# Edge softmax by products over edges, an attention table in two parts, and a new order of the last layers, in a four-layer graph network

## The chip, the cores and the metric

The kernel runs on one core of one Trainium2 chip. The core has five engines with instruction streams of their own, which wait for one another by semaphores: TensorE (PE in the profile; PEld are its weight loads), VectorE (DVE), ScalarE (ACT), GpSimd (POOL) and SyncE (SP). SP and POOL here mostly issue transfers between DRAM and on-chip memory (SBUF); a queue's transfers are issued in program order, so one that has to wait holds up those behind it. Products of TensorE land in PSUM. The metric is the device time of one execution in microseconds (us); less is better.

## The reference, cut to what matters

Input `x` is [128, 64, 256]: 128 samples of 64 nodes with 256 features. Four layers each compute `x = layernorm(x + layer(x))`: two graph convolutions with windows of LSTMs, a graph convolution with batch norm, attention over 512 random edges, and a convolution in the eigenvector basis of the graph. The change is in the last two and in the tables of the third:

```
def _L2_gnn_ref(H, W_lin, W_val, a, W_out, A0, src, dst):     # 4 heads of 64, E = 512 edges
    Xq, Xv = (H @ W_lin.T), (H @ W_val.T)                     # each as [bt, 64, 4, 64]
    e = einsum('behd,hd->beh', leaky_relu(Xq[:, src] + Xq[:, dst], 0.2), a)
    e = e + log(A0[src, dst] + EPS)
    m = segment_max(e_t, src, 64)                             # per source node
    ex = exp(e_t - m[src])
    denom = segment_sum(ex, src, 64)
    attn = ex / denom[src]
    Y = segment_sum(attn * Xv[:, dst], src, 64)
    return Y @ W_out.T

def _L3_gnn_ref(features, A, W1, b1, W2, b2):
    _, U = eigh(normalized Laplacian of A)
    h = relu(U.T @ features @ W1 + b1)
    return U @ (h @ W2 + b2)
```

## The kernel before, in words

**Where things are.** X, the activations, stays in SBUF as [128, 64 tiles, 256]: a tile holds two samples (b = 0, 1), each with its 64 nodes on 64 partitions. All layers update X in place. `Norm` (L1221) is the residual and layer norm: `add` adds a result to two tiles and takes their statistics on VectorE; when four tiles are gathered, `flush` works out the scale and shift in some ten small operations (a square root of them on ScalarE, L1214) and ScalarE applies them, one instruction a tile (L1253).

**Attention, scores.** `scores()` is a generator of 32 steps; step k covers two tiles. A step has two half-steps c = 0, 1 (two of the four heads each): TensorE gathers source plus target by a product with the 0/1 table GG (`l`, L1903), ScalarE copies it out (L1909), VectorE makes the leaky ReLU (L1910), TensorE multiplies by the attention vector into the score tile `sc` (L1857), maps the next tiles to queries and values (`m`, L1880), and transposes those after (L1869). Values are stored to DRAM by SP, one `xv` store a step (L1884). Sixteen steps are a half: 32 tiles give a score tile of 128 rows (16 units of two tiles, two parities, two heads) by 512 edges for each c.

**Softmax of a half.** Edges are sorted by source, so the reference's segments are runs of columns. `softmax(half, es)` runs on VectorE: add the edge logs `lg`; for each c two scans over the 512 columns (forward and backward, L1932 and L1933) spread each run's maximum, with `br` breaking them at the runs' ends; subtract; exponential on ScalarE; two more scans (L1937, L1938) with the 0/1 table `kp` (1 where a column goes on with the run) spread each run's sum; a reciprocal of 128x512 (L1940); a product (L1941). Each `yield` is a place where the hand-written order can put other work.

**Table.** `table` transposes the result into edges by rows on TensorE (L1951), copies it to `at` on ScalarE in an order that puts each parity's 128 values side by side (L1952), and scatters 4 x 128 edge rows of 1 KB with four indirect transfers from POOL (L1955) into `attn_d`, a DRAM table [64 x 64 pairs, 256] that was filled with zeros long before (L1740). Each scatter waits until the one before has landed. `fetch(half)` reads that table back into `M2` [128, 64, 128] with eight transfers from SP (L1964); each row that is read contiguously is one pair's 128 floats of one parity, 512 B.

**Values.** `values()` is a generator of 33 calls. Call k loads the next unit (`load`: ScalarE copies a slice of M2 to `mc`, L1971; POOL fetches the stored values `xr`, L1974), multiplies attention by values for two tiles (`mixed`, L1986), copies `yT` (L1989), and does the output product of the tiles before (`po`, L2007) with `ln.add`. So every second call closes four tiles of X with a flush. Calls that load units 0 to 15 read the first half's M2, the others the second's.

**The last layer.** `blocks()` is a generator of 19 calls; call q does basis(q) (L2074: four tiles times U, ScalarE copies `ag`, POOL adds the constant `cb` to X at L2078), first_map(q − 1) (L2084), back(q − 2) (L2092) and second_map(q − 3) (L2101, then `ln3.add` and the store of four finished tiles by SP, L2103). basis(q) needs tiles 4q to 4q + 3 of X after attention's norm. `constants()` prepares `cb` and `nb` from four small loads (L2046 to L2052), once (L2057).

**The order** is written out by hand in `run(...)`, which takes one step of each generator named; the streams of the engines follow it, with the scheduling tools of the language free to move little. In before, the softmax of half 0 is laid beside five steps of scoring, `table` follows, and `fetch(0)` one step later; four steps of scoring on come seven pairs of a scoring step and a value call. After scoring: the loads of the last layer's weights, `constants()`, value calls mixed with the softmax of half 1 and blocks, and the table of half 1; then

```
fetch(1)
run(*[val, val, l3] * 10)
run(*[val] * 2, *[l3] * (NT // 4))
```

The source's own line numbers are those of the profile.

Of the kernel before, what the change touches and what calls it, by code (L numbers as in the profile page):

```python
# [1259 lines left out]
def tile_adj_resnorm(ctx: ExitStack, tc: tile.TileContext, I: dict, out: bass.AP, layers: int = 4):  # L1260
# [45 lines left out]
    EDGE = (("GG", E), ("lg", E), ("kp", E + 1), ("br", E + 1), ("ix", 4))  # L1306
# [4 lines left out]
    attn_d = dram.tile([N * N + E, 2 * P], F32, tag="attn_d", name="attn_d")  # L1311

    def edge_tables(t):
        at, o = 0, {}
        for name, w in EDGE:
            o[name] = t[:, at : at + w]
            at += w
        return [o[k] for k in ("GG", "lg", "kp", "br")] + [o["ix"].bitcast(I32)]
# [73 lines left out]
    def sort_edges(gk, gp):  # L1392

        def gt_(tag, shape, dtype=F32, bufs=None):
            return gk.tile(shape, dtype, tag=tag, name=tag, bufs=bufs)

        edge_s = gt_("edge_s", [P, WE])
        GG, lg, kp, br, ix = edge_tables(edge_s)
# [54 lines left out]
        v.memset(kp, 0.0)  # L1453
        v.tensor_tensor(kp[:, 1:E], row[0][:, 1:], row[0][:, : E - 1], ALU.is_equal)
        v.tensor_scalar(br, kp, 1.0, 1e30, ALU.subtract, ALU.mult)
        OS, OD = gt_("kr", [P, E]), gt_("ef", [P, E])
        v.tensor_scalar(OS, row[0], pmod, None, ALU.is_equal)
        v.tensor_scalar(OD, row[1], pmod, None, ALU.is_equal)
        v.tensor_tensor(GG, OS, OD, ALU.add)
        ps = gp.tile([P, 512], F32, tag="ps", name="ps")  # L1460
# [278 lines left out]
    for z in attn_d[: N * N, :].rearrange("(k p a) q -> k p (a q)", p=P, a=4):  # L1739
        nc.sync.dma_start(z, zero)  # L1740
# [65 lines left out]
    with ExitStack() as l2:  # L1806
# [9 lines left out]
        GG, lg, kp, br, ix = edge_tables(edge_s)  # L1816
# [16 lines left out]
        kf, kb, bf, bb = kp[:, :E], kp[:, 1:], br[:, :E], br[:, 1:]  # L1833
# [6 lines left out]
        es, soft = [[], []], []  # L1840
# [83 lines left out]
        def softmax(half, es):  # L1924

            for c in range(2):
                es.append(sm.tile([P, E], F32, tag="se", name="se"))
                v.tensor_tensor(es[c], sc[half][c], lg, ALU.add)
            yield
            for c, e in enumerate(es):  # L1930
                f = sm.tile([P, 2, E], F32, tag="sf", name="sf", bufs=1)[:, 0, :]
# [5 lines left out]
                v.tensor_tensor_scan(f, kf, e, 0.0, ALU.mult, ALU.add)  # L1937
                v.tensor_tensor_scan(f[:, ::-1], kb[:, ::-1], f[:, ::-1], 0.0, ALU.mult, ALU.max)  # L1938
                yield
                v.reciprocal(f, f)  # L1940
                v.tensor_tensor(e, e, f, ALU.mult)  # L1941
                yield

        def table(es):

            at = sm.tile([P, 2, E], F32, tag="sf", name="at", bufs=1).rearrange(
                "p a b -> p (a b)").rearrange("p (k b u c i) -> p k b u c i", k=4, b=2, u=HU, c=2)
            for c, e in enumerate(es):
                ps = pp.tile([P, 512], F32, tag="m", name="m")
                for k in range(4):  # L1950
                    te.transpose(ps[:, k * P : (k + 1) * P], e[:, k * P : (k + 1) * P], ident)  # L1951
                s.copy(at[:, :, :, :, c, :].rearrange("p k b u i -> p (k b) i u"),  # L1952
                       ps.rearrange("p (k i u) -> p k i u", i=4, u=HU))
            for k in range(4):
                nc.gpsimd.indirect_dma_start(  # L1955
                    out=attn_d[:, :], out_offset=bass.IndirectOffsetOnAxis(ap=ix[:, k : k + 1], axis=0),
                    in_=at[:, k].rearrange("p b u c i -> p (b u c i)"), in_offset=None)

        def fetch(half):

            M2[half] = lw.tile([P, N, P], F32, tag="M2", name="M2", bufs=2)
            for n0 in range(0, N, 16):
                for b in range(2):
                    nc.sync.dma_start(  # L1964
                        M2[half][b * N : (b + 1) * N, n0 : n0 + 16, :],
                        attn_d[: N * N, b * P : (b + 1) * P].rearrange("(d n) q -> d n q", n=N)[:, n0 : n0 + 16, :])
# [44 lines left out]
        def run(*steps):  # L2011
            for x in steps:
                next(x, None)
# [7 lines left out]
        lw, sm = own1(valuing, name="l2w", bufs=1), own1(valuing, name="l2s", bufs=2)  # L2021
        ln = Norm(nc, sm, X, 4, act=True)
        val = values()
        soft += [softmax(h, es[h]) for h in range(2)]
# [14 lines left out]
        with tc.tile_pool(name="l3w", bufs=1) as l3w, tc.tile_pool(name="l3s", bufs=2) as s3, tc.tile_pool(  # L2039
            name="l3p", bufs=6, space=PSUM  # L2040
        ) as p3:
            bank = lambda: p3.tile([P, 512], F32, tag="ps", name="ps")
            w1 = l3w.tile([P, 2, P], F32, tag="w31", name="w31")
            nc.sync.dma_start(w1, kio(I["W31"]))
            w2 = l3w.tile([P, D], F32, tag="w32", name="w32")
            nc.sync.dma_start(w2, I["W32"])  # L2046
            b1 = l3w.tile([P, 1], F32, tag="b31", name="b31")
            nc.sync.dma_start(b1, I["b31"])
            nb1 = l3w.tile([P, P], F32, tag="nb1", name="nb1")
            nc.sync.dma_start(nb1, I["b31"].rearrange("p o -> (p o)").partition_broadcast(P))  # L2050
            cb = l3w.tile([P, D], F32, tag="cb", name="cb")
            nc.sync.dma_start(cb, I["b32"].partition_broadcast(P).rearrange("p o d -> p (o d)"))  # L2052

            def constants():
                v.tensor_scalar(nb1, nb1, -1.0, None, ALU.mult)
                ps = bank()
                te.matmul(ps[:, :D], b1.to_broadcast([P, P]), w2, start=True, stop=True)  # L2057
                te.matmul(ps[:, D : D + 1], bdut, ones[:, 0:1], start=True, stop=True)
                ru = l3w.tile([P, 1], F32, tag="ru", name="ru")
                v.tensor_copy(ru, ps[:, D : D + 1])  # L2060
                v.tensor_tensor(cb, cb, ps[:, :D], ALU.add)
                v.tensor_scalar(cb, cb, ru, None, ALU.mult)

# [121 lines left out]
```

## Time and profile before

| what | value |
|---|---|
| median of 3 runs | 2470.07 us (2470.02 to 2470.59) |
| the profiled execution | 2471.62 us, of which the span of the trace 2469.8 |
| granted TensorE clock, mean | .977 |
| ScalarE busy | 964.4 us (39%) |
| GpSimd busy | 75.1 us (3%) |
| DMA | 101.25 MB, mean 41 GB/s |
| softmax of half 0, first to last VectorE operation | about 2050 to 2090 us |
| scores end | about 2256 us |
| softmax of half 1 | 2252.8 to 2290.3 us |
| eight indirect scatters, issue each | .96 to 1.02 us; landing 2.4 to 3.6 us |
| sixteen reads of the table, landing each | 5.5 to 14.6 us |

Times in the timeline are from the start of the span. A timeline row has a start, a duration, engine, line, operation, destination and sources, a count where several of a kind follow one another, and in brackets how long the engine had been idle and what released it. A windows row has a length, and then, in the order PE, PEld, DVE, ACT, POOL, the busy us in it with the number of instructions; after these the granted clock of TensorE (1.00 is full), the mean busy share of the 16 DMA engines and the GB/s moved. A tile row has the shortest, median and longest duration in ns, and the first and last start.

### The profile page before, as it was taken

How to read it: one execution, taken by the hardware profiler on the slowest of the kernel's cores; microseconds unless marked ns; L12 is line 12 of the kernel's file. 1: busy time of each engine (PE TensorE's matmuls, PEld its weight loads, DVE VectorE, ACT ScalarE, POOL GpSimd, SP SyncE). 2: the span in 40 equal slices, each digit the busy share in tenths (PEclk: the TensorE clock that was granted, in tenths of full speed). 3: DMA queues.
4: the chain of work that ended last, by engine and by line, in shares of the span. 5: the costliest groups of instructions: out<-in, count | busy, mean ns of one | idle time of the engine just before them, and what ended most of it. 6: DMA issues, size and time to landing. Idle time of an engine off the chain costs nothing. (4 is left out here: it accounts for less than half of the span.)

```text
span 2469.8 us, 29195 instructions
## 1 busy us (share of the span) xinstructions
PE 2300.6 (93%) x9016; PEld 1232.0 (50%) x9016; DVE 1794.5 (73%) x8172; ACT 964.4 (39%) x1678; POOL 75.1 (3%) x115
## 2 busy tenths in 40 slices
PE   7999999999999999999999988998978888899797
PEld 5544654444664444655445634554433333246786
DVE  3667766677977798877889877777846768456577
ACT  1322222242332343322333322334447665456575
POOL 0000000000000000000000000000000000002331
PEclk9999999999999999999999999999989999999899
DMA  6000000000100001000001001002210000511622
GB/s 213 18 18 35 1 34 1 34 26 9 52 35 1 35 35 51 1 35 1 35 34 52 1 29 36 35 1 111 75 37 22 22 22 22 98 35 47 133 87 74
DMA packets 59861, 101.25 MB, mean 41 GB/s; under 512 B 5137, under 2 KB 40081, under 8 KB 59441
## 3 DMA queue, kind: packets, MB, share of 16 engines
q1 hardware_dynamic: 54624, 88.83, 11.3%
q0 software_dynamic: 3216, 10.21, 1.5%
q8 instruction: 72, 1.18, 0.2%
q14 instruction: 93, 0.75, 0.1%
q10 hardware_dynamic: 1856, 0.28, 0.1%
HBM read 67.84 MB, written 31.46 MB: 40 GB/s over the span
## 5 line engine op out<-in xcount | busy, mean ns | idle before, releaser
L1587 PE MATMUL pq<-H,wi 128*128 128x512 f32 (+1 forms) x2016 | 826.8, 546 | 5.1 <-DVE H L1612 5.1
L1593 ACT ACTIVATE gate<-pq,bl 128x512 f32<-128x512 f32 (+1 forms) x504 | 317.7, 635 | 845.9 <-PE pq L1591 663.1
L1587 PEld LDWEIGHTS pq<-H,wi 128*128 128x128 f32 x2016 | 373.4, 190 | 333.2 <-issue 260.1
L1591 PE MATMUL pq<-lh,wh 128*128 128x512 f32 (+1 forms) x1152 | 474.8, 538 | 24.9 <-DVE lh L1608 24.6
L1591 PEld LDWEIGHTS pq<-lh,wh 128*128 128x128 f32 x1152 | 216.1, 192 | 223.2 <-issue 138.7
L1910 DVE SCALAR_TENSOR_TENSOR xs<-xs 128x512 f32<-128x512 f32 x256 | 166.2, 681 | 67.6 <-ACT xs L1909 66.9
L1909 ACT COPY xs<-l 128x512 f32<-128x512 f32 x256 | 137.2, 589 | 85.4 <-PE l L1903 45.4
L1903 PE MATMUL l<-edge_s,xq 64*128 64x512 f32 x512 | 140.3, 648 | 16.4 <-ACT xs L1909 11.6
L1733 PE MATMUL ps<-at,w 128*128 128x512 f32 x256 | 116.7, 607 | 9.2 <-ACT at L1729 7.7
L1880 PE MATMUL m<-wqv,xT 128*128 128x512 f32 x256 | 123.1, 618 | 1.7 <-ACT xs L1909 0.9
L1750 PE MATMUL ps<-h,w 128*128 128x512 f32 x256 | 114.6, 606 | 5.9 <-ACT h L1745 5.9
L1605 ACT ACTIVATE gate<-lc 128x1024 f32<-128x1024 f32 (+1 forms) x72 | 69.0, 958 | 119.6 <-DVE lc L1600 61.8
L1253 ACT ACTIVATE X<-X,ln_sh,ln_rs 128x256 f32<-128x256 f32 x192 | 99.1, 590 | 25.5 <-DVE ln_sh L1249 19.7
L142 DVE COPY AQR<-eps 64x192 f32<-64x192 f32 (+1 forms) x125 | 35.1, 281 | 101.9 <-PE eps L148 101.7
L1237 DVE BATCH_NORM_STATS2 ln_st<-X 128x6 f32<-128x256 f32 x256 | 98.9, 415 | 2.2
L1880 PEld LDWEIGHTS m<-wqv,xT 128*128 128x128 f32 x256 | 46.0, 192 | 78.1 <-issue 58.6
L1903 PEld LDWEIGHTS l<-edge_s,xq 64*128 64x128 f32 x512 | 47.9, 196 | 69.9 <-issue 35.6
L1750 PEld LDWEIGHTS ps<-h,w 128*128 128x128 f32 x256 | 48.9, 194 | 66.2 <-issue 57.5
L1733 PEld LDWEIGHTS ps<-at,w 128*128 128x128 f32 x256 | 47.6, 192 | 65.7 <-issue 48.6
L1974 POOL DMA_DIRECT2D xr<-xv x32 | 17.6, 550 | 2053.7 <-DVE xs L1910 1836.4
L1857 PE MATMUL sc<-xs,az 128*32 128x512 f32 x512 | 68.2, 605 | 3.0 <-DVE xs L1910 3.0
L1602 DVE TENSOR_TENSOR gate<-gate 128x1024 f32<-128x1024 f32 (+1 forms) x36 | 38.0, 1055 | 42.7 <-ACT gate L1593 42.7
(557 smaller groups left out, 3222.2 us busy)
## 6 DMA issues: line engine op xcount, KB each, us to landing
wi<-in_WihT_dram SPq DMA_DIRECT2D x16, 1024.0 KB, 4.8
wh<-in_WhhT_dram SPq DMA_DIRECT2D x12, 1024.0 KB, 6.5
X<-in_x_dram SPq DMA_DIRECT2D x16, 512.0 KB, 9.2
xd<-X SPq DMA_DIRECT2D x16, 512.0 KB, 2.6
X<-xd SPq DMA_DIRECT2D x16, 512.0 KB, 3.2
xv<-xv SPq DMA_DIRECT2D x32, 256.0 KB, 2.0
xr<-xv POOLq DMA_DIRECT2D x32, 256.0 KB, 2.9
M<-attn_d SPq DMA_DIRECT2D x16, 512.0 KB, 11.2
```

The source lines that it names most:

```text
L1237: nc.vector.bn_stats(st, self.X[:, k, :])
L1253: nc.scalar.activation(x, x, AF.Identity, bias=sh[:, k : k + 1], scale=rs[:, k : k + 1])
L1587: te.matmul(ps, wi[:, kk, o * P : (o + 1) * P], at(kk, k), start=(kk == 0), stop=(k == 0 and kk == 1))
L1591: te.matmul(ps, wh[:, kk, o * P : (o + 1) * P], hst[:, kk, :M], start=False, stop=(kk == 1))
L1593: s.activation(gates[gt][:, c, :M], ps, AF.Tanh if gt == 2 else AF.Sigmoid, bias=bl[:, p - 1, o : o + 1])
L1605: s.activation(gg, cs2, AF.Tanh)
L1733: te.matmul(ps, w1[:, k, c * P : (c + 1) * P], at[:, k, :], start=(k == 0), stop=(k == 1))
L1750: te.matmul(ps, w2[:, k, c * P : (c + 1) * P], h[:, k, :], start=(k == 0), stop=(k == 3))
L1880: te.matmul(ps, xT[:, i, c, :], wqv[:, c, :], start=(c == 0), stop=(c == 1))
L1903: mms.append(te.matmul(pl[i][:, b, :], xq[i][r, c * P : (c + 1) * P], GG[r, :], start=True, stop=True))
L1909: taken.append(s.copy(x, pl[i][:, b, :]))
L1910: ready.append(v.scalar_tensor_tensor(x, x, 0.2, x, ALU.mult, ALU.max))
```

## The change

*Tables of the edges* (set up early, in layer 0): `kp` goes; `OS` comes, 0/1 of source node (128 rows, the 64 nodes twice) by 512 edges, which GG was already made from, and `OE`, its transpose in four pieces of 128 edges by 64 nodes, made by four transposes and a copy.

*Softmax*: the maxima stay as scans. The sums and their inverses are made after the transposition: the exponentials are transposed as before and copied to `eT` unpermuted; four products over edges with OE give the sums per node [64, 128]; VectorE bounds them from below by .5 and takes their reciprocal; four products with OS spread these back over the edges; VectorE multiplies `eT` by that, writing `at` in the permuted order. `table` is now the end of the same generator, which has eight steps in all.

*Table*: one DRAM table for each parity, each [pairs, 128]. There are eight scatters with rows of 512 B, in two chains. `fetch` reads, for a target node, 16 pairs x 128 floats that lie together: 8 KB.

*Order*: softmax 0 is laid beside six steps of scoring with `fetch(0)` after the sixth; three steps of scoring and `constants()` (its loads now go out before the steps around the middle of scoring, and its weights have a pool of their own), then the seven pairs as before. After scoring, seven blocks instead of six come before the first value call that reads the second table, and the repeated period starts with the block.

```diff
-    EDGE = (("GG", E), ("lg", E), ("kp", E + 1), ("br", E + 1), ("ix", 4))
+    EDGE = (("GG", E), ("OS", E), ("lg", E), ("br", E + 1), ("OE", 4 * N), ("ix", 4))
-    attn_d = dram.tile([N * N + E, 2 * P], F32, tag="attn_d", name="attn_d")
+    attn_d = [dram.tile([N * N + E, P], F32, tag=f"attn_d{b}", name="attn_d") for b in range(2)]
...
+        for k in range(4):
+            te.transpose(ps[:, k * N : (k + 1) * N], OS[:N, k * P : (k + 1) * P], ident[:N, :N])
+        v.tensor_copy(OE, ps[:, : 4 * N])
...
-    for z in attn_d[: N * N, :].rearrange("(k p a) q -> k p (a q)", p=P, a=4):
-        nc.sync.dma_start(z, zero)
+    for b in range(2):
+        for z in attn_d[b][: N * N, :].rearrange("(k p a) q -> k p (a q)", p=P, a=8):
+            nc.sync.dma_start(z, zero)
...
                 s.activation(e, e, AF.Exp)
                 yield
-                v.tensor_tensor_scan(f, kf, e, 0.0, ALU.mult, ALU.add)
-                v.tensor_tensor_scan(f[:, ::-1], kb[:, ::-1], f[:, ::-1], 0.0, ALU.mult, ALU.max)
-                yield
-                v.reciprocal(f, f)
-                v.tensor_tensor(e, e, f, ALU.mult)
-                yield
...
+            byedge = []
+            for e in es:
                 ps = pp.tile([P, 512], F32, tag="m", name="m")
                 for k in range(4):
                     te.transpose(ps[:, k * P : (k + 1) * P], e[:, k * P : (k + 1) * P], ident)
-                s.copy(at[:, :, :, :, c, :].rearrange("p k b u i -> p (k b) i u"),
-                       ps.rearrange("p (k i u) -> p k i u", i=4, u=HU))
+                eT = sm.tile([P, 4, P], F32, tag="sf", name="eT")
+                s.copy(eT.rearrange("p k r -> p (k r)"), ps)
+                ps = pp.tile([P, 512], F32, tag="m", name="m")
+                for k in range(4):
+                    te.matmul(ps[:N, :P], OE[:, k * N : (k + 1) * N], eT[:, k, :], start=(k == 0), stop=(k == 3))
+                rc = sm.tile([N, P], F32, tag="rc", name="rc")
+                v.tensor_scalar(rc, ps[:N, :P], 0.5, None, ALU.max)
+                v.reciprocal(rc, rc)
+                byedge.append((eT, rc))
+                yield
...
+            for c, (eT, rc) in enumerate(byedge):
+                ps = pp.tile([P, 512], F32, tag="m", name="m")
+                for k in range(4):
+                    te.matmul(ps[:, k * P : (k + 1) * P], OS[:N, k * P : (k + 1) * P], rc, start=True, stop=True)
+                v.tensor_tensor(at[:, :, :, :, c, :].rearrange("p k b u i -> p (k b) i u"),
+                                eT.rearrange("p k (i u) -> p k i u", u=HU).rearrange("p k (b i) u -> p (k b) i u", b=2),
+                                ps.rearrange("p (k i u) -> p k i u", i=4, u=HU), ALU.mult)
+                yield
             for k in range(4):
-                nc.gpsimd.indirect_dma_start(
-                    out=attn_d[:, :], out_offset=bass.IndirectOffsetOnAxis(ap=ix[:, k : k + 1], axis=0),
-                    in_=at[:, k].rearrange("p b u c i -> p (b u c i)"), in_offset=None)
+                for b in range(2):
+                    nc.gpsimd.indirect_dma_start(
+                        out=attn_d[b][:, :], out_offset=bass.IndirectOffsetOnAxis(ap=ix[:, k : k + 1], axis=0),
+                        in_=at[:, k, b].rearrange("p u c i -> p (u c i)"), in_offset=None)
+            yield
...
-                        attn_d[: N * N, b * P : (b + 1) * P].rearrange("(d n) q -> d n q", n=N)[:, n0 : n0 + 16, :])
+                        attn_d[b][: N * N, :].rearrange("(d n) q -> d n q", n=N)[:, n0 : n0 + 16, :])
...
         run(*[sc_] * (HU - NQ + 2))
-        for _ in range(3):
-            run(sc_, soft[0], soft[0])
-        run(soft[0], sc_)
-        table(es[0])
-        run(sc_)
+        run(*[sc_, soft[0]] * 5, sc_, soft[0], soft[0])
         fetch(0)
-        run(*[sc_] * 4)
+        run(*[sc_] * 3)
+        constants()
         run(*[sc_, val] * 7)
...
-            constants()
-            run(val, soft[1], val, soft[1], l3, soft[1], val, soft[1], l3, soft[1], val, soft[1], l3)
-            table(es[1])
-            run(val, l3)
+            sf = soft[1]
+            run(val, sf, val, l3, sf, val, sf, l3, sf, val, sf, l3, sf, sf, val, l3)
             fetch(1)
-            run(*[val, val, l3] * 10)
-            run(*[val] * 2, *[l3] * (NT // 4))
+            run(val, val, l3, val, l3, l3, val, val, val)
+            run(*[l3, val, val] * 7, val, *[l3] * (NT // 4))
```

The loads of `w31`, `w32`, `b31`, `nb1` and `cb` and the body of `constants()` are the same text, moved ahead of the scoring steps. The first step of each softmax (the addition of the logs) is taken inside `scores()` when a half's last score product is made, as before.

More of the change, by code (lines that the diff above doesn't have):

```diff
@@ L1922, in scores, with softmax @@
                 yield
-        def softmax(half, es):
+        def softmax(half):
+            es = sm.tile([P, 2, E], F32, tag="se", name="se", bufs=1)
+            es = [es[:, c, :] for c in range(2)]
             for c in range(2):
-                es.append(sm.tile([P, E], F32, tag="se", name="se"))
                 v.tensor_tensor(es[c], sc[half][c], lg, ALU.add)
             yield
-            for c, e in enumerate(es):
-                f = sm.tile([P, 2, E], F32, tag="sf", name="sf", bufs=1)[:, 0, :]
+            for e in es:
+                f = sm.tile([P, E], F32, tag="sf", name="sf")
                 v.tensor_tensor_scan(f, bf, e, -1e30, ALU.add, ALU.max)
@@ new lines, in constants @@
+        def constants():
+            v.tensor_scalar(nb1, nb1, -1.0, None, ALU.mult)
+            ps = pp.tile([P, 512], F32, tag="m", name="m")
+            te.matmul(ps[:, :D], b1.to_broadcast([P, P]), w2, start=True, stop=True)
+            te.matmul(ps[:, D : D + 1], bdut, ones[:, 0:1], start=True, stop=True)
+            ru = l3w.tile([P, 1], F32, tag="ru", name="ru")
+            v.tensor_copy(ru, ps[:, D : D + 1])
+            v.tensor_tensor(cb, cb, ps[:, :D], ALU.add)
+            v.tensor_scalar(cb, cb, ru, None, ALU.mult)
@@ L2031, in tile_adj_resnorm @@
+        soft += [softmax(h) for h in range(2)]
+        run(*[sc_] * (HU - NQ + 2))
+        run(*[sc_, soft[0]] * 5, sc_, soft[0], soft[0])
         fetch(0)
-        run(*[sc_] * 4)
+        run(*[sc_] * 3)
+        constants()
         run(*[sc_, val] * 7)
         scoring.close()
-        with tc.tile_pool(name="l3w", bufs=1) as l3w, tc.tile_pool(name="l3s", bufs=2) as s3, tc.tile_pool(
-            name="l3p", bufs=6, space=PSUM
-        ) as p3:
+        scoring.close()
+        lw = own1(valuing, name="l3m", bufs=1)
@@ L2042, in tile_adj_resnorm @@
+        with tc.tile_pool(name="l3s", bufs=2) as s3, tc.tile_pool(name="l3p", bufs=6, space=PSUM) as p3:
             bank = lambda: p3.tile([P, 512], F32, tag="ps", name="ps")
[L2043 to L2062, printed above, removed]
```

40 lines of the change are left out of this document (25 added, 15 removed).

## The prediction, made before the changed kernel had run

> **What bounds the kernel now.** I read the page's first part, then the busy windows over the last 470 us, then the timeline where a window shows TensorE (PE) short of work, and last the tiles that the change removes.
>
> ```profile
> span 2469.8 us, 29195 instructions
> PE 2300.6 (93%) x9016; PEld 1232.0 (50%) x9016; DVE 1794.5 (73%) x8172; ACT 964.4 (39%) x1678; POOL 75.1 (3%) x115
> ```
>
> PE is the bound over the whole span. The change acts only between about 2050 and 2440 us, and windows (length; busy us of PE, PEld, DVE, ACT, POOL; granted clock; DMA share; GB/s) show what bounds there:
>
> ```profile
> 2060.00:2070.00 10.00, 7.44 (x34) 2.50 (x27) 9.93 (x12) 3.87 (x8) 0.00 (x0) 1.00 0.00 0
> 2120.00:2130.00 10.00, 9.97 (x45) 3.40 (x44) 5.84 (x9) 5.34 (x12) 0.00 (x0) 1.00 1.23 190
> 2130.00:2140.00 10.00, 1.83 (x4) 0.52 (x4) 0.02 (x1) 1.81 (x2) 0.00 (x0) 0.71 0.99 179
> 2255.00:2265.00 10.00, 6.94 (x73) 5.09 (x74) 6.84 (x15) 6.00 (x8) 1.08 (x2) 0.77 0.36 99
> 2290.00:2300.00 10.00, 9.44 (x70) 8.82 (x70) 3.20 (x11) 6.51 (x11) 4.27 (x5) 0.66 0.19 66
> 2330.00:2340.00 10.00, 4.60 (x68) 4.02 (x69) 0.00 (x0) 8.15 (x14) 1.09 (x2) 0.50 0.72 179
> 2370.00:2380.00 10.00, 10.00 (x114) 8.69 (x113) 7.73 (x30) 8.06 (x19) 2.02 (x5) 1.00 0.20 56
> ```
>
> In the first softmax VectorE (DVE) bounds; at 2130 and 2330 the table's transfer does; at 2255 a late constant; at 2290 the half clock after a stall; from 2345 on PE is full and nothing else is waited for.
>
> **The change, part by part.** Gains and losses are in us of the profiled execution, 2471.62 (span 2469.8).
>
> *First softmax.* Per half and channel c, four DVE operations go:
>
> ```profile
> L1937 DVE TENSOR_TENSOR_SCAN sf<-edge_s,se x4: 1214/1216/1278, 2057.1 to 2283.1; 128x512 f32<-128x512 f32 x4
> L1940 DVE RECIPROCAL sf<-sf x4: 3345/3353/3353, 2061.3 to 2285.6; 128x512 f32<-128x512 f32 x4
> ```
>
> 1.22 + 1.21 (the second scan) + 3.35 + .68 (product) = 6.46, four times 25.8 in all. Added on DVE: a reciprocal of 64x128, a quarter of the columns, 3.35/4 = .84; a maximum of about .2; a product from PSUM, not shown in this order of access, between .68 (L1941) and 1.3 (the double). DVE keeps .68 + 1.22 + 1.22 + .69 = 3.81 per c for the maxima. The burst per half-step of scoring falls to 3.8, against some 2.1 that DVE leaves free (5.84 of 10 busy in an undisturbed window, half-step 5.1). Between 2050 and 2090 PE stood 5.6 idle and lost 1.6 on one half-clocked product (L1903 3.58 for 1.99): 7.2. I leave 2 of it: −5.2 (bounds −7.2 and −2). PE gains per c four products over OE (moving 128) and four over OS; eight such passes took .9 to 1.06 (L2092), a group of four some .5, but the scheduler of PE is full there, and each carries a weight load: I take .9 for each four, 3.6 for two c (bounds 1.9 and 4.2). The OE products stand one instruction behind the ACT copy (.59) they need: 2 x .5 = 1. Constants, moved into scoring: PE 1.19 (L2057). Together −5.2 + 3.6 + 1 + 1.2 = +0.6.
>
> *First table.*
>
> ```profile
> 2113.21 16.37 SPq L1964 DMA_DIRECT2D M<-attn_d  x8
> 2129.68 3.12 SPq L1884 DMA_DIRECT2D xv<-xv  x2
> 2138.19 2.00 ACT L1971 COPY mc<-M 128x512 f32<-128x512 f32 x2 [9.01 <-DMA xv<-xv]
> 2141.22 3.53 PE L1903 MATMUL l<-edge_s,xq 64*128 64x512 f32 x8 [9.39 <-ACT xs L1909]
> ```
>
> Eight issues in rows of 512 B land after 25 us; ACT's mc sits in the order ahead of the copies of scoring, so DVE and PE starve. Cost: 9.39 idle and 1.5 to 2.2 at half clock, 11. In after the rows are 8 KB on both sides. The nearest large rows here are the zero fill's (4 KB):
>
> ```profile
> 1690.00:1694.00 4.00, 3.00 (x7) 0.97 (x6) 3.55 (x10) 1.40 (x3) 0.00 (x0) 1.00 1.02 405
> ```
>
> 405 GB/s for 190: 4.2 MB in 10.4; by 274 GB/s of the load of x (1 KB rows) 15.3; at the old rate 25. I take 14. The table is ready later: the last product stands at half-step 44 (the copies of before at 40), mc at 50 (45.5). So there are 6 x 5.1 = 30.6 from product to mc; needed are 1.3, the scatters and 14. Scatters took 11.6 from 2101.64 to 2113.21, each waiting for the one ahead to land (2.4 to 3.6). Eight now run in two independent chains: POOL issues 8 x .99 = 7.9, chains as long as before: 11.6 (bounds 8 and 14). 26.9 of 30.6: hidden, −11. If the old rate holds: 37.9, 7.3 of stall stay. SP has xv22 and xv23 ahead of the table now; xv24, still behind it, is read at half-step 51, as late as mc itself. Zero fills keep their bytes; OE's four transposes lie in layer 0, some .6 on PE, left out.
>
> *Behind the scores, to the second table.* Three losses of PE:
>
> ```profile
> 2260.64 1.19 PE L2057 MATMUL ps<-w,b 128*128 128x256 f32 x2 [2.80 <-DMA cb<-in_b_dram]
> 2290.31 0.66 PE L1951 MATMUL m<-ident,se 128*128 128x128 f32 x4 [2.86 <-DVE se L1941]
> 2335.37 3.26 PE L1986 MATMUL m<-mc,xr 64*64 64x64 f32 x64 [9.68 <-ACT mc L1971]
> ```
>
> Each is followed by half clock: 6 us of it (3.0 lost) after the first, some 7 (3.4) after the second, 7 (3.5) after the third. 2.7 + 3.0, 2.9 + 3.4, 9.7 + 3.5: 25.2. The five loads move far ahead on SP, past xv14 to xv31, and land during scoring; the reciprocal goes; and a seventh block (6.3 of PE: 1.79 + 1.79 + .9 + 1.8) fills the wait for the table. Table and PE: the scatters start near 2284 (2292.6 less the stalls gone, plus the products), + 14 with four X+=cb of POOL (L2078, .7) among them, + 16 for the transfer with an out store between: 2314. PE's own work reaches to 2325. Hidden with 11 to spare, at the old rate with none or little. Back come 3.6 of products less 1.2 of constants, 2 for copies and reciprocals that PE waits for, and 1.5 because block 6 asks for the tiles of the call just ahead of it: −25.2 + 2.4 + 3.5 = −19.3 (bounds −25 and −10).
>
> *The repeated period.* It was two value calls and a block, and still is, but blocks now run one period ahead: basis(q) reads X that the norm flushed one call ago, where there were three calls between. One period of before (starts, durations):
>
> ```profile
> 2349.43 1.99 PE L2007 MATMUL ps<-wo,yT 128*128 128x256 f32 x8
> 2353.66 2.08 ACT L1253 ACTIVATE X<-X,ln_sh,ln_rs 128x256 f32<-128x256 f32 x4
> 2354.09 1.95 PE L2074 MATMUL ps<-bda,X 128*128 128x128 f32 x16
> 2355.63 0.20 ACT L1214 ACTIVATE is_s<-is_t 128x4 f32<-128x4 f32 x1
> 2357.67 2.08 ACT L1253 ACTIVATE X<-X,ln_sh,ln_rs 128x256 f32<-128x256 f32 x4 [0.88 <-DVE ln_sh L1249]
> ```
>
> The first row is the product whose flush the second group of X closes; the group ends 10.3 after it. The basis at 2354.09 reads older tiles; in after it reads these. By this row its last tile comes at 2359.75 + .45 against an end of 2355.88: +4.3 a period. ACT's order in after has is_s of this norm ahead of the first group of X: is_t is there at 2353.7, X 2353.9 to 2356.0 and 2356.0 to 2358.1, basis to 2358.6: +2.6. Seven periods: +18 (bounds 17 and 30). Queued behind the waiting basis are first_map, back, second_map and the next mixed; ACT's ag and mc wait for it too.
>
> Sum: 0.6 − 11 − 19.3 + 18 = −11.7. 2471.62 − 11.7 = 2459.9; the median shown is 1.55 below that execution: 2458.4, say 2458.
>
> The Trainium skill, DMA: Bandwidth & Descriptors, Specifications, puts line rate at transfers of 512 B and more. The old rows had just that and moved 190 GB/s where 4 KB rows moved 405, so the row disagrees; by the rule wider rows bring nothing and the sum would be about 2470.
>
> The Trainium skill, TensorE: Matmul & The Clock Gate, What's actually happening, halves the clock after an idle window of some 3.4 us. Rows above have it after 2.80 and 2.86; by the rule the stalls of 2.6 stay at full clock (2458), by the rows some may not.
>
> **Rivals.**
> *The period's wait takes the gain (slower).* Place: basis behind L1253, seven times. For it: idles of 2.8 halved the clock here, and DVE's small norm operations stretch to .65 beside POOL (L1217 at 2356.30). Against: PE's idle of 2.5 at 2064 left the clock at 1.00. Price: 4.3 x 7 = 30 in place of 18, and 1.6 (one product at half clock, as at 2072) x 7 = 11: 2458 + 12 + 11 = 2481. It decides from 29.7/7 = 4.2 a period on.
> *The period absorbs it.* If the norm's chain shortens once PE no longer paces it, to 5 in all: 2445. Against: its ten links are serial.
> *Rows are not the limit.* 64 partitions a transfer set the rate, as before: 7.3 + 2 of half clock come back at the first table, up to 3 at the second: 2470. For it: the DMA share was 1.23 already, above that of the zero fill; against: the zero fill's 405.
>
> **How the numbers follow.** Forecast .45 (own range 2448 to 2468), slower rival .22, absorbed .15, rows .12, mixtures .06. A measurement tells some 0.2% (5 us) from no change: faster is below 2465, slower above 2475. Faster .45 x .95 + .15 + .05 = .63; same .10 (rows, the forecast's edge); slower .27. The range takes in the absorbed case and the slow one: 2438 to 2481.
>
> **What would show it.** ACT's mc of call 0 without a wait for M, PE without a gap near 2130 and 2330; M's landing at 14 or less for the whole table, over 270 GB/s; no wait of PE for cb; DVE without a full 10 us in the softmax. The period: PE L2074 waiting for X L1253 seven times, 2 to 3 us each, period 14.4 for 11.85, clock 1.00. The forecast is wrong if that wait is above 4.2, if PE shows .5 of clock there, or if there is none; or if M still lands after 25.

## The result, and the profile after

The changed kernel takes 2480.67 us in the median of 7 runs (2474.55 to 2484.2); the kernel before, on the same chips, 2470.07 (2465.53 to 2471.99). The ratio is 1.0042, 95% interval 1.0028 to 1.0056: slower, where 2458 had been forecast. The profiled execution is the shortest of the seven, 2474.55 with a span of 2472.8, so it is only 2.9 above the profiled one of before. Where the other six lose up to 9.65 us more, no trace shows.

The page's header for the changed kernel:

```profile
span 2472.8 us, 29353 instructions
PE 2306.5 (93%) x9084; PEld 1235.3 (50%) x9084; DVE 1775.9 (72%) x8169; ACT 961.8 (39%) x1678; POOL 83.5 (3%) x123
```

VectorE lost 19 us of work and PE gained 6. Below, the stages in order; the numbers of lines in the changed kernel differ from those of before by some six to twenty (the scoring products `l` are L1909, the basis L2091).

**Constants.** In the timeline, VectorE stands at the first operation on the constants for the load of `nb`, and the score product behind it waits:

```profile
2010.79 0.43 SPq L2050 DMA_DIRECT2D nb<-in_b_dram  x1
2015.10 0.23 DVE L2055 TENSOR_SCALAR nb<-nb 128x128 f32<-128x128 f32 x1 [3.94 <-DMA nb<-in_b_dram]
2016.58 1.87 PE L1863 MATMUL sc<-xs,az 128*32 128x512 f32 x8 [2.39 <-DVE xs L1916]
```

The call stands far behind in the program (its products run at 2154), but VectorE's operation depends on the load alone and was scheduled right behind it; the load lands 4.3 us after its issue, and VectorE stands for 3.94 of them. The eight score products then take 1.87 instead of 1.06: half clock. The scoring step is 3.8 longer.

**First table.** The transfer, the copy that reads it, and PE behind it:

```profile
2137.88 5.56 SPq L1982 DMA_DIRECT2D M<-attn_d  x8
2159.44 2.05 ACT L1989 COPY mc<-M 128x512 f32<-128x512 f32 x2 [4.25 <-DMA xv<-xv]
2164.03 0.66 PE L1875 MATMUL m<-ident,X 128*128 128x128 f32 x4 [2.54 <-ACT xv L1889]
```

The windows while it runs (columns as before):

```profile
2138.00:2148.00 10.00, 9.97 (x48) 3.55 (x44) 5.68 (x10) 5.58 (x12) 0.00 (x0) 1.00 0.93 211
2148.00:2158.00 10.00, 9.97 (x50) 3.77 (x46) 6.07 (x12) 3.88 (x9) 0.00 (x0) 1.00 1.00 219
```

From first issue to `mc` 21.5 us, at 211 to 219 GB/s; before it was 25 at 190. PE's 9.39 shrink to 2.54. (The bracket names a store of xv; `mc` reads M, and the last queue event ahead of it happened to be that store.)

**Behind the scores.** One window over the same work of both kernels, from the last value call beside scoring to the basis behind call 18; the changed kernel does one block more in it. Before:

```profile
2252.49:2342.13 89.64, 73.76 (x705) 64.84 (x701) 59.59 (x167) 55.19 (x104) 27.66 (x39) 0.85 0.51 109
```

After:

```profile
2248.59:2333.42 84.83, 79.49 (x806) 68.13 (x802) 59.08 (x179) 55.64 (x108) 33.85 (x47) 0.98 0.43 109
```

PE's idle time falls from 15.9 to 5.3, of which 2.62 is the second softmax and 1.28 the table, and the clock rises from .85 to .98. With the extra block's 6.3 the stage gains 4.8 + 6.3 = 11.1.

**The period.** One period in the timeline, then PE's waits from 2330 on (total, times, longest):

```profile
2345.26 0.31 ACT L1214 ACTIVATE is_s<-is_t 128x4 f32<-128x4 f32 x2
2346.59 4.04 ACT L1253 ACTIVATE X<-X,ln_sh,ln_rs 128x256 f32<-128x256 f32 x8 [1.01 <-DVE ln_sh L1249]
2349.20 0.71 PE L2091 MATMUL ps<-bda,X 128*128 128x128 f32 x4 [2.43 <-ACT X L1253]
2363.57 0.71 PE L2091 MATMUL ps<-bda,X 128*128 128x128 f32 x4 [2.44 <-ACT X L1253]
2379.56 0.71 PE L2091 MATMUL ps<-bda,X 128*128 128x128 f32 x4 [2.44 <-ACT X L1253]
2393.93 0.71 PE L2091 MATMUL ps<-bda,X 128*128 128x128 f32 x4 [2.44 <-ACT X L1253]
```

```profile
PE ps L2091 <- ACT X L1253: 16.5, 8, 2.4
```

The two square roots go together and the eight applications of scale and shift in one row, so the flushed tiles come last, and the basis waits 2.4 us for the first of them. The starts are 14.37, 15.99 and 14.37 apart, against 11.85 before. The long one is the one in whose window the clock falls:

```profile
2360.00:2370.00 10.00, 7.56 (x76) 7.25 (x75) 3.19 (x16) 6.65 (x15) 3.41 (x5) 0.83 0.32 104
2370.00:2380.00 10.00, 7.56 (x92) 6.20 (x91) 7.42 (x32) 5.51 (x13) 1.09 (x2) 1.00 0.21 54
```

Both windows hold the same 2.44 of idle time; after one of the waits PE runs at half clock for some 3.4 us, after the other not. A period is 14.4, or 16.0 when the clock drops.

What tells the two apart can be read from the trace. The granted clock changes only on a grid of 3.41 us: the two drops of this stretch, at 2364.87 and 2409.24, are 13 x 3.41 apart, and each lasts one such step. Steps of the grid around two of the waits:

```profile
2361.46:2364.87 3.41, 1.30 (x11) 1.31 (x12) 1.07 (x6) 3.41 (x8) 0.97 (x2) 1.00 0.54 162
2364.87:2368.28 3.41, 3.41 (x18) 3.41 (x17) 0.00 (x0) 2.68 (x6) 2.42 (x4) 0.50 0.22 74
2375.11:2378.52 3.41, 2.01 (x38) 1.46 (x36) 3.24 (x20) 2.47 (x7) 0.58 (x2) 1.00 0.27 77
2378.52:2381.93 3.41, 2.37 (x21) 2.37 (x22) 0.00 (x1) 3.26 (x9) 1.50 (x3) 1.00 0.77 233
```

The first wait lies with 2.11 of its 2.44 in one step (PE is busy for 1.30 of 3.41), and the step behind it is at half clock. The second is split by the grid, 1.40 and 1.04, and no drop follows. All twelve waits of 2.43 or 2.44 in this trace and in that of experiment 3 go this way: the five with 2.11 to 2.44 in one step dropped the clock, the seven with at most 1.84 did not. The drops of experiment 3 (2352.95, 2383.67 and 2428.05) are 9 and 13 steps apart. So it is the place of a wait on the grid that decides here, and the grid lies differently against the program in each trace. Idle time in a step is not the whole rule, for in experiment 2 two steps with 1.2 and 1.5 of it were followed by half clock as well; and no run moved a wait on the grid alone.

### The profile page after: what moved, and what is told of

Same layout as the page of the kernel before. It is cut to its first block, busy times and chain, and to the rows that moved or that the text cites. A ratio compares the mean times of both kernels' runs of the same rounds, so it can differ in the third digit from the quotient of the medians.

```text
span 2472.8 us, 29353 instructions
## 1 busy us (share of the span) xinstructions
PE 2306.5 (93%) x9084; PEld 1235.3 (50%) x9084; DVE 1775.9 (72%) x8169; ACT 961.8 (39%) x1678; POOL 83.5 (3%) x123
## 5 line engine op out<-in xcount | busy, mean ns | idle before, releaser
L1909 PE MATMUL l<-edge_s,xq 64*128 64x512 f32 x512 | 139.3, 635 | 6.6 <-ACT xs L1915 4.4
L1909 PEld LDWEIGHTS l<-edge_s,xq 64*128 64x128 f32 x512 | 47.5, 192 | 58.8 <-issue 36.1
L129 DVE SCALAR_TENSOR_TENSOR CS<-GA,qE 64x1 f32<-64x1 f32 x294 | 61.8, 210 | 9.8
## 6 DMA issues: line engine op xcount, KB each, us to landing
M<-attn_d SPq DMA_DIRECT2D x16, 512.0 KB, 10.5
```

The source lines that it names most:

```text
L1909: mms.append(te.matmul(pl[i][:, b, :], xq[i][r, c * P : (c + 1) * P], GG[r, :], start=True, stop=True))
```

## The experiments

Ratios are to the kernel before, with 95% intervals. Each kernel is compared with 9 to 21 runs of before from its chip; the experiments ran on three chips, so kernels of different chips are best compared by their ratios. Executions differ ahead of the change too: one and the same transposition early in scoring (`m` from `X`) starts at 1901.58 in the profiled execution of the changed kernel, at 1905.82, 1906.87, 1904.32 and 1901.51 in those of experiments 1, 3, 5 and 9, whose sources differ from it only behind that point. A difference of some 4 us between two kernels with five runs each is therefore at the edge of what these runs can tell.

**1. The margin restored.**

```diff
-            run(*[l3, val, val] * 7, val, *[l3] * (NT // 4))
+            run(*[val, val, l3] * 7, val, *[l3] * (NT // 4))
```

> The changed kernel with two value calls ahead of each block in the repeated period again, so that three calls lie between a flush and the basis that reads it; all else as changed. Theory A (the period's wait took the gain: 16.5 us of waits and some 3 to 10 us of half clock after them): no PE wait for X L1253 in the period, period 11.9 instead of 14.4, and a time of 2455 to 2462 us, below the kernel before. Rival B (the wait is only shifted, the norm's chain or ScalarE paces the period either way, and the loss lies in the products and the constants): above 2472.

Measured: 2460.12 (2455.99 to 2464.68), ratio .9965 (.9954 to .9977): faster than before, and 20.6 under the changed kernel. From 2335 on PE waits for X once only, in the tail:

```profile
PE ps L2091 <- ACT X L1253: 0.6, 1, 0.6
```

Theory A holds: one line of the order turned the gain into a loss.

**2. The new order alone, in the kernel before.**

```diff
-            run(*[val, val, l3] * 10)
-            run(*[val] * 2, *[l3] * (NT // 4))
+            run(val, val, l3, val, l3, l3, val, val, val)
+            run(*[l3, val, val] * 7, val, *[l3] * (NT // 4))
```

> The kernel before with nothing but the new order behind the second fetch: seven blocks ahead of the second table and blocks first in the period. Theory A: the wait for the second table shrinks by a block's 6.3 us and a little half clock (a gain of 6 to 9), the period loses 17 to 25: 2478 to 2489 us. Rival B: the order alone gains the 6 to 9 and loses nothing: 2461 to 2464.

Measured: 2492.1 (2491.94 to 2493.29), ratio 1.0092 (1.0078 to 1.0107). The loss is above A's upper end. The waits are 17.9; the rest is the clock, which falls in nearly every period here. Two of its windows:

```profile
2370.00:2410.00 40.00, 32.31 (x284) 29.97 (x285) 15.46 (x66) 23.32 (x47) 10.88 (x16) 0.83 0.24 73
2410.00:2450.00 40.00, 33.97 (x293) 31.08 (x292) 19.70 (x78) 17.81 (x39) 6.30 (x9) 0.87 0.11 34
```

.17 x 40 + .13 x 40 = 12 us at half clock, of which a part lies in the waits themselves. By the starts of the basis, six periods take 98.7 (2356.51 to 2455.22) for 71.1 in before: 27.6 lost, 17.1 of it waits and some 10.5 the clock. PE's wait for the second table shrinks from 9.7 to 3.4, as A had it, and 27.6 less 6 to 9 is near the 22 measured.

**3. The constants' first operation held to its place.**

```diff
-            v.tensor_scalar(nb1, nb1, -1.0, None, ALU.mult)
+            after(v.tensor_scalar(nb1, nb1, -1.0, None, ALU.mult), taken)
```

> The changed kernel with VectorE's first operation on the constants (nb, L2055) held until after the copies of the scoring step ahead of constants(); its load is unchanged. Theory C (VectorE stood 3.9 us at 2011 for the load of nb, the products behind waited 2.4 and ran 1.6 longer at half clock): 3.7 us less than the changed kernel on the same chip. Rival D (that stop is made up by slack later in scoring): no difference beyond the scatter of the changed kernel, 2474 to 2484.

Measured: 2474.62 (2470.96 to 2480.08), ratio 1.0019 (1.0011 to 1.0028), 6.1 under the changed kernel; the ranges of runs overlap, the intervals of the ratios only touch. The wait of 2.39 is gone from the trace, and the scoring step takes 13.27 where the changed kernel had 17.03: C holds for the step. Its profiled execution, at 2479.1 longer than its median and than the changed kernel's 2474.55, shows how executions scatter. It reaches the scoring 5.3 later (1906.87 for 1901.58), at the first table a step takes 14.2 for 11.2 with half clock in it, and in the period, with the same eight waits of 16.5, the clock drops three times instead of two:

```profile
2352.11 0.71 PE L2091 MATMUL ps<-bda,X 128*128 128x128 f32 x4 [2.43 <-ACT X L1253]
2368.11 0.71 PE L2091 MATMUL ps<-bda,X 128*128 128x128 f32 x4 [2.44 <-ACT X L1253]
2382.46 0.71 PE L2091 MATMUL ps<-bda,X 128*128 128x128 f32 x4 [2.43 <-ACT X L1253]
2398.46 0.71 PE L2091 MATMUL ps<-bda,X 128*128 128x128 f32 x4 [2.44 <-ACT X L1253]
```

16.00, 14.35, 16.00. That the size at the median is 6 and not 3.8 is within this scatter.

**4. The old table in the changed kernel**: one of 256 columns, scatters of 1 KB, 512 B rows in the fetch.

```diff
-    attn_d = [dram.tile([N * N + E, P], F32, tag=f"attn_d{b}", name="attn_d") for b in range(2)]
+    attn_d = dram.tile([N * N + E, 2 * P], F32, tag="attn_d", name="attn_d")
...
-                        attn_d[b][: N * N, :].rearrange("(d n) q -> d n q", n=N)[:, n0 : n0 + 16, :])
+                        attn_d[: N * N, b * P : (b + 1) * P].rearrange("(d n) q -> d n q", n=N)[:, n0 : n0 + 16, :])
```

> The changed kernel with the old table: one of 256 columns, four scatters of 1 KB rows in one chain, 512 B rows in the fetch. Theory E (the wide rows moved 4.2 MB in 21.5 instead of 25 us only, so they are worth that difference at each table): the first value call's copy is ready some 3 us later, PE waits 5 to 7 at the first table instead of 2.5 and some more at the second; 4 to 9 us above the changed kernel. Rival F (the layout does not matter, position does): same time and same landing.

Measured: 2484.36 (2481.42 to 2486.7), ratio 1.0058 (1.0045 to 1.0071): 3.7 above the changed kernel, just under E's lower end; the two intervals overlap. In the trace `mc` starts 25.0 after the first issue, where it was 21.5, so F's "same landing" falls. PE's longest wait for xv goes from 2.5 to 6.2 and the one for the second table from 1.3 to 3.0. The table in two parts, rows and scatters together, is worth about 4 us.

**5. Both repairs**: the two diffs of 1 and 3 together.

> The changed kernel with both repairs: two value calls ahead of each block in the repeated period, and VectorE's first operation on the constants held until its place in scoring. Theory A and C (two separate losses, 20.6 and 6.1 by the runs before): they add up, 2452 to 2457. Rival (the second only showed because the period's wait passed its half clock on): no better than the margin alone, 2460.

Measured: 2457.29 (2455.42 to 2461.14), ratio .9950 (.9936 to .9963). It is the upper end of the first theory and 2.8 under the margin alone (2.6, each against before on its own chip), with overlapping intervals. The stall is gone from the trace (a scoring step of 13.27 for 17.1 in 1); that the two repairs add is likely, but the times do not show it.

**6. The old softmax in the new order.** Sums by scans, reciprocal and product on VectorE, then the old transposes and permuted copies as the last of eight steps; all else as in 5.

```diff
-            byedge = []
-            for e in es:
...
+                v.tensor_tensor_scan(f, kf, e, 0.0, ALU.mult, ALU.add)
+                v.tensor_tensor_scan(f[:, ::-1], kb[:, ::-1], f[:, ::-1], 0.0, ALU.mult, ALU.max)
+                yield
+                v.reciprocal(f, f)
+                v.tensor_tensor(e, e, f, ALU.mult)
+                yield
```

> Both repairs, and the softmax of before (sums by scans, reciprocal of 128x512 on VectorE, transposes and permuted copies behind them) in the new order of steps, one step of it to a step of scoring; table in two parts as changed. Theory G (the new spacing of the steps, not the products, is what freed PE in the first softmax: VectorE leaves 2.1 us free in each half-step, 25 in twelve, and the old softmax needs 20.5): PE saves the 4.4 to 5 us of products a half, waits little more: equal to or up to 8 us less than with both repairs alone. Rival H (the products free VectorE and that is what PE sees): 5 to 12 us more than with both repairs alone.

Measured: 2457.14 (2456.21 to 2458.0), ratio .9946 (.9933 to .9960): the same as with the products, so H's 5 to 12 us are not there at the median. PE's busy time on the two pages is

```profile
PE 2296.2 (94%) x9016; PEld 1227.8 (50%) x9016; DVE 1795.0 (73%) x8172; ACT 963.3 (39%) x1678; POOL 83.9 (3%) x123
```

for the old softmax and 2305.9 for the products: 9.7 of PE work are saved, and waited away elsewhere (PE for `xs` up to 6.3, for `mc` 3.4, for the softmax 3.4; with the products 1.1, none and 2.6). G's lower end did not come. Experiment 10 comes back to this.

**7. 128 partitions a transfer.** The two parts in one DRAM tile, eight transfers of 128 partitions with 4 KB rows; all else as in 5.

```diff
-            for n0 in range(0, N, 16):
-                for b in range(2):
+            for n0 in range(0, N, 8):
+                nc.sync.dma_start(
+                    M2[half][:, n0 : n0 + 8, :],
+                    attn_t.rearrange("(b r) q -> b r q", b=2)[:, : N * N, :].rearrange(
+                        "b (d n) q -> b d n q", n=N)[:, :, n0 : n0 + 8, :])
```

> Both repairs, and the table's two parts laid in one DRAM tile, so that each of the eight transfers of a fetch fills all 128 partitions with 4 KB rows in place of 64 with 8 KB rows; the eight scatters may then go one after another (some 12 us later). Theory I (64 partitions a transfer hold the rate near 230 GB/s): over 300 GB/s in the windows of the fetch, the last of eight landing under 15 us after the first issue, in place of 21.5. Rival J (reading scattered DRAM pages, or something on the memory's side, sets it): 210 to 250 GB/s again, 20 us or more. The time is not the test: 2452 to 2470 by how the scatters queue.

Measured: 2602.3 (2600.04 to 2604.93), ratio 1.0535 (1.0518 to 1.0551). Neither theory: a window in the middle of the fetch shows

```profile
2170.00:2180.00 10.00, 0.00 (x0) 0.00 (x0) 0.00 (x0) 0.00 (x0) 0.00 (x0) 0.50 0.13 52
```

.13 of 16 engines is two engines, 26 GB/s each by this row. The transfer's outermost dimension is the 2 of the parities, and the pad rows between the parts keep it from merging with the 64 rows. The question of the partitions stayed open, so:

**8. The same with the parts back to back** (pad rows behind both; one dimension of 128 rows).

```diff
-                    attn_t.rearrange("(b r) q -> b r q", b=2)[:, : N * N, :].rearrange(
-                        "b (d n) q -> b d n q", n=N)[:, :, n0 : n0 + 8, :])
+                    attn_t[: 2 * NR, :].rearrange("(p n) q -> p n q", n=N)[:, n0 : n0 + 8, :])
```

> As the run with 128 partitions a transfer, but with the two parts of the table back to back in the DRAM tile (pad rows behind both), so that the 128 rows of a transfer are one dimension of even stride and not two by 64. In the run before the 2 as outermost dimension put each transfer on two DMA engines (share .13, 52 GB/s). Theory I (64 partitions a transfer hold the rate near 230): share near 1, over 300 GB/s, all eight landed within 15 us of the first issue; time 2452 to 2460 though the eight scatters go in one chain. Rival J (the memory's side holds it): 210 to 250 GB/s, 20 us or more; time 2460 to 2475, for the scatters' chain costs some 8 us more at each table.

Measured: 2461.91 (2459.78 to 2466.81), ratio .9970 (.9960 to .9979). The fetch runs at

```profile
2150.00:2155.00 5.00, 3.53 (x18) 1.06 (x14) 0.00 (x0) 0.00 (x0) 0.00 (x0) 1.00 1.02 417
```

and `mc` starts 13.3 after the first issue. So theory I: not the rows but the 64 partitions held the changed kernel's fetch near 220. The time is in rival J's span all the same: the eight scatters went in one chain, 22.3 us from the first to the table's first read in place of 12.2, and PE stood 9.6 at the first table.

**9. First value call a scoring step later**, on 5.

```diff
-        run(*[sc_] * 3)
+        run(*[sc_] * 4)
         constants()
-        run(*[sc_, val] * 7)
+        run(*[sc_, val] * 6)
...
-            run(val, sf, val, l3, sf,
+            run(val, val, sf, val, l3, sf,
```

> Both repairs, and the first value call one scoring step (10.2 us) later, with six of them beside scoring and one more behind it. Theory K (2.5 us of PE wait and a little more at the first table go, nothing else moves): 2 to 4 us less than with both repairs alone. Rival L (the call that leaves scoring, whose PE work was already full there, adds ScalarE and POOL work to the second softmax and delays its table): equal or slower.

Measured: 2453.22 (2451.66 to 2455.13), ratio .9931 (.9917 to .9944): 4.1 under 5, the lowest of all, and 16.7 under before on its chip. PE's wait at the first table only goes from 2.10 to 1.57, with a group at half clock behind it in both, so K's 2 to 4 us by that wait are not what the trace shows.

**10. The old softmax with the value call later**: the diffs of 6 and 9 on 5.

> Both repairs, the old softmax in the new spacing, and the first value call one scoring step later. Theory G (the products bring PE work that pays for what they free): the same as with the products, 2451 to 2455. Rival H2 (the old softmax only kept up because its table was waited for anyway): 2456 or more. Rival G2 (without the first table's wait the 9 us of products a kernel show): 2445 to 2450.

Measured: 2458.17 (2455.95 to 2459.19), ratio .9947 (.9933 to .9961). By the median H2: 12.7 under before on its chip, where 9 is 16.7 under, with intervals that just overlap. H2's reason is not in the traces, though: with the old softmax PE waits at the first table in both places of the value call, 6.28 in 6 and 5.03 here, and with the products 2.10 in 5 and 1.57 in 9. From one and the same transposition of scoring (it starts at 2036.78 in 5, 2032.87 in 6, 2033.98 in 9, 2036.12 here) to the end the profiled executions take 416.9 and 421.5 in 5 and 6, 416.6 and 420.6 in 9 and 10. So in both pairs the products are some 4 us faster behind that point, and the equal medians of 5 and 6 can come from what lies ahead of it. By the same count the later value call is worth .3, not 4.1. These are single executions: that the products pay is likely, what the later call is worth stays open.

**11. The order alone**: as 6, with the old table by the diff of 4.

> Both repairs and the old softmax, and the old table too: 256 columns, four scatters in a chain, 512 B rows. What is left of the change is the order: spacing of the softmax's steps, later fetch and value calls, early constants, seven blocks ahead. Theory M (order and constants carry most of the gain; the wide rows are worth some 4): 2459 to 2463. Rival N (the two-part table carries half of it or more): 2464 to 2470.

Measured: 2461.61 (2458.3 to 2462.81), ratio .9960 (.9944 to .9975): M. Against before on their own chips 11 gains 9.2, 6 gains 12.8 and 9 gains 16.7. Spacing, position and early constants thus give some 9; the table in two parts some 3.6 (the 3.7 of experiment 4); the products and the later value call the other 4. The last two steps are at the edge of the scatter.

**12. The constants alone, in the kernel before**, with the hold of 3 and the five loads where the changed kernel has them.

```diff
         run(*[sc_] * 4)
+        constants()
         run(*[sc_, val] * 7)
...
-            constants()
             run(val, soft[1], val, soft[1], l3,
```

> The kernel before with only the constants moved: loads ahead of the middle of scoring, constants() in scoring with VectorE's first operation on them held to its place, second M2 in a pool of its own. The prediction had 2.7 of wait and 3.0 of half clock gone for 1.2 of PE work in scoring. Theory O (those gains are kept): 2464 to 2467. Rival P (PE then waits as much longer for the second softmax or the second table, both of which VectorE, POOL and the transfer pace): 2468 to 2471.

Measured: 2467.73 (2465.75 to 2468.26), ratio .9986 (.9977 to .9995): some 3 gained of the 4.5 that O wanted, between the spans of O and P. The trace has part of it come back as longer waits, PE for `mc` 10.7 (9.7 before) and for the softmax 4.0 (2.9).

## Why the prediction was wrong

The offset between the two profiled executions, read at the transposition that opens each scoring step and at the basis of each block, gives each term of the sum its measured size:

| step of the prediction | forecast | measured |
|---|---|---|
| constants in scoring | +1.2 | +4.6 (3.76 stall, .89 products) |
| first softmax, VectorE's burst | −5.2 | −5.8 |
| products, transposes and their copies | +4.6 | +7.3 |
| first table | −11 | −8.5 (−11.0, and 2.5 back) |
| behind the scores | −19.3 | −11.1 |
| the period, seven times | +18 | +18.9 (15.4 of waits, 3.2 clock) |
| start and end of the stretch | 0 | −2.4 |
| sum, profiled execution | −11.7 | +3.0 |

Of the −2.4 at the start and end, 1.35 stands ahead of the transposition at 1901.58 (1902.93 in before). The table covers 14.7 of the 22.3 between the 2458.4 of the sum and the 2480.67 measured. The other 7.7 is where the two profiled executions lie against their medians: 6.1 below in the changed kernel, 1.55 above in before.

The burst was near: 5.8 for 5.2. The table's stall went as worked out, 11.0. The period's place, cause and wait were right, 2.44 for the 2.6 of the sum (.77 in the first period), from the row of the norm's chain with the square root moved ahead. That the total of 18.9 is so near to 18 is partly luck: the waits came to 15.4, and 3.2 are half clock, which the sum did not have.

**The steps that failed.** *The constants.* "Constants, moved into scoring: PE 1.19" counted PE alone and left VectorE's operation on `nb` and its load without a place; experiment 3 gives 6 for it, the trace 3.8. In the trace that operation stands ahead of the one that the score products wait for.

*Behind the scores*, −19.3, is the largest single miss, 8. Two things made it. First, PE's own work: the sum let it grow by 2.4 beyond the extra block, and counted at full clock it grew by 7.7 (63.8 to 77.8, less the block's 6.3). The products are 4.2 of that (4.9 as they ran, four groups of 1.1 to 1.5) where the sum had 3.6; the constants take off .6 instead of 1.2; .75 are `mixed` products of the next call, which in before stand behind the window; some 3.4 are spread over the rows of value calls and blocks, and their cause stays open. Second, waits and half clock: the sum took off 21.7 of them (25.2 less the 3.5 that come back), the window 18.8: 10.5 of idle time, and 8.3 of clock, with PE busy at half clock for 3.4 us instead of 19.9. The second softmax kept a wait of 2.62 with half clock behind it. "Hidden with 11 to spare" rested on a transfer of 14 to 16; at 220 GB/s with an out store between it took 26, from 2300.3 to `mc` at 2326.2, which used up the 11: PE waited 1.28. Experiment 12 shows the same from the other side: a wait taken away there comes back in part at the next thing waited for.

*The first table.* The 14 us were read from the zero fill's 405 GB/s, which writes from 128 partitions with 4 KB rows; the fetch has 64 partitions. Experiment 8 shows which of the two mattered: 417 GB/s with 128 partitions and rows half as wide. The rival "rows are not the limit" named this mechanism, at .12; in size it lay between the two, 21.5 for 14 and 25.

*The period's clock.* The sum left it out, and the slower rival carried it, at 1.6 a period. That is what a long period shows, 15.99 − 14.37 = 1.62. The profiled execution has it twice in the seven, and experiment 2 loses some 10.5 by it. The rival's point against itself, an idle of 2.5 that left the clock at 1.00, is the grid again: that wait of 2.56 is split by it, 1.40 and 1.16, and the next one of 2.41, with 2.25 in one step, dropped the clock at 2072.70. The seven runs' spread, 9.65, would be six such drops, and their granted clocks go from .982 (2474.55) to .978 (2484.2). But the executions shown above differ by 5.4 ahead of the scoring, too, so where the median loses its 6 against the profiled run is open; no trace of that run exists.

Where the slower rival was wrong: it needed 4.2 a period. The wait stayed at 2.4, and a period is 2.5 or 4.1 too long by whether the clock drops. The profiled execution came out slower because the gains ahead, 35.5 in the forecast (burst, table, stage behind the scores), were 25.4, and constants and products cost 6.1 more.

The rule of 512 B (the Trainium skill, DMA: Bandwidth & Descriptors, Specifications) was nearer than the forecast and still not the point: 8 KB rows moved 219 GB/s for the 190 of 512 B rows, and 128 partitions 417. The idle window of 3.4 us (the Trainium skill, TensorE: Matmul & The Clock Gate, What's actually happening) is no bound here: waits of 2.44 halved the clock in two of seven periods, in experiment 2 waits of 2.7 to 2.9 in five of six.

## What to carry to other kernels

A repeated order that keeps its members but starts with another one can take the slack out of a dependency that spans several calls: count the calls between writer and reader after the change, not the members of the period. An operation that depends on a load alone can be scheduled right behind the load, far ahead of where its call stands; give it an order. A short wait of PE costs its length and, by where it falls, some 1.6 us more at half clock; in a repeated period that is met many times over. Before two variants that differ by some microseconds are ranked, compare their traces from a common point: here what lay ahead of the change differed by as much.

## What the runs showed of the hardware that was not expected

A transfer whose outermost dimension is 2 ran on two of the 16 DMA engines, 52 GB/s (experiment 7). Eight transfers of 512 KB to 64 partitions each moved 211 to 219 GB/s at a share near 1.0, to 128 partitions 417 at a share of 1.02 (experiment 8). Waits of 2.44 us, the same each time, halved TensorE's clock in some periods and left it in others of one execution; the drops lie on a grid of 3.41 us, and came behind the five of twelve such waits that fell with 2.11 or more into one step of it.
